# A perceiver layer on one NeuronCore: the loads' order at the start, and the experts' second products with tokens on the rows

## The chip, the core and the metric

The kernel runs on one NeuronCore of a Trainium2 chip. The core has five engines with instruction queues of their own: TensorE (PE; its weight loads are listed apart as PEld), VectorE (DVE), ScalarE (ACT), GpSimd (POOL) and SyncE (SP). They work from SBUF, 128 partitions (rows) wide; TensorE writes to PSUM, eight banks from which VectorE and ScalarE read. DMAs move data between HBM and SBUF; here SP and ACT issue them. An engine takes its instructions in the order of its queue, and a DMA-issuing instruction that has to wait holds up what is behind it in that queue.

The metric is the device time of one execution in microseconds (us).

## What is computed

32 sequences of 64 tokens and 256 features (2048 tokens) attend to a context of 1601 keys each, then to themselves with a Gaussian-like span per head, and then pass through a feed-forward part with one shared expert and eight routed ones. In the reference's words, shortened:

```python
x = x + xattn(layernorm(x), ctx, ctx, mask, ...)      # 16 heads of 16; q, k, v, o with biases
x = x + attn(layernorm(x), W_span, W_val, W_out)       # scores = -soft * (pos - mean)**2
x = x + ffn(layernorm(x), ...)

# ffn, over the tokens n = 0 .. 2047
shared = silu(xf @ sw1 + sb1) * (xf @ sw3 + sb3) @ sw2 + sb2
out = 0
for k in range(2):
    e = (n * 11 + k * 7919) % 8                        # the expert is a function of n % 8
    out += gelu(xf @ w1[e] + b1[e]) @ w2[e] + b2[e]
ffn = (shared + out / 2) / 2
```

As the expert depends on n % 8 alone, the tokens fall into eight classes r of 256 tokens each, and a class has two experts. All arithmetic is in float32.

## The kernel before, in words

**Start.** `cst` (constants: the identity matrix among them), `cols` (biases as columns) and the first tile of x are asked for on SP; `load_square` asks for the query, key and value weights and others on ACT (L122), eight loads in all with `bo_row` and `woP` (L127, L129). Then SP asks for the mask (L328) and, in `load_context(0)`, for the first sequence's context in four pieces of 496, 372, 372 and 361 keys (`GROUPS`, L404). Tiles named `ct` hold such pieces, in five buffers. At any time up to eight of the loads can be under way; a ninth waits until an earlier one has landed.

**Cross attention.** From L571 to `order.close()` (L671) the order on PE, DVE, ACT and POOL is the order of the program text (`manual_schedule`); what is traced outside of this region may be set between its instructions by the framework's scheduler, which models each engine's time and places an instruction when its inputs would be there. `query_steps` (L370) is a generator in five steps: statistics of the tile (DVE, `spread_of`), normalising (two ACT operations), transposes on PE (L170) and a copy (L377), the query products (L382) with four ACT copies into `qbd` (L390), and a bias addition (L397). The first four steps run ahead of everything (L581 to L583). `project_keys` (L413) makes a group of keys: PE products (L419) and an ACT copy with bias into `kT` (L423). `scores` (L446) makes scores (L454), DVE adds the mask to them into `prob` (L463), `maximum` keeps a running maximum (L484). Then POOL subtracts it (L515), ACT takes exponentials (L520), and `values` (L522) multiplies by the values `v` (L530), which `project_values` makes (L435, L441). A half (one sequence, eight of the heads) is worked on while the next half's scores are made. When two sequences are done, `span_steps` (L178) takes their tile through the second attention, spread over the following stretches, with operations on all four engines (L182 to L312), and writes it to `x_kept` in HBM (L306) and, normalised and transposed, to `xfT`.

**Feed-forward.** The pools of the attention are closed, and new pools `ffn`, `hid` and three PSUM pools use their memory anew; a new tile waits only for those old tiles that lie under it (`reuse_waits="tile"`). Tiles lie in a pool in the order in which the program first asks for them. SP asks for the weights (L685). The shared expert's first products run in four quarters of the tokens, interleaved with the last tile's `span_steps` (the agenda); the last quarter (L715) waits until that tile is done, as it needs the whole of `xfT`. `expert_hidden` (L741) makes a class's hidden values for its two experts (L748, L755). `expert_out` (L759) forms the second products with features on the rows: the weights are the stationary operand, 256 tokens of the class the moving one; DVE scales by 0.25 and adds the column bias `ybias` (made at L699 to L708) into `yT`, with a stride of eight tokens (L770). At the end each of the 16 token tiles is turned back by two PE transposes (L783), added to the kept x (`xe`, one load at L738) by DVE (L785) and stored (L786).

This region has no order of its own in the text: the scheduler lays it.

Of the kernel before, what the change touches and what calls it, by code (L numbers as in the profile page):

```python
# [15 lines left out]
F32 = mybir.dt.float32  # L16
U8 = mybir.dt.uint8
AF = mybir.ActivationFunctionType
ALU = mybir.AluOpType
# [3 lines left out]
P = 128  # L23
S = 64
D = 256
H = 16
# [27 lines left out]
B_2 = B_1 + 2 * E  # L54
B_S2 = B_2 + TOPK * 2 * E
B_V = B_S2 + 2
# [3 lines left out]
def expert_of(k: int, r: int) -> int:  # L60

    return (r * PRIME + k * HASH_OFF) % E
# [16 lines left out]
def perceiver_kernel(ctx: ExitStack, tc: tile.TileContext, a: dict[str, bass.AP], out: bass.AP):  # L79
# [14 lines left out]
    def mm_bank(name: str):  # L94
        return ps_mm.tile([P, 512], F32, tag="mm", name=name)
# [3 lines left out]
    nc.sync.dma_start(out=cst, in_=a["consts"])  # L99
# [6 lines left out]
    nc.sync.dma_start(out=cols, in_=a["cols"])  # L106
# [7 lines left out]
    def load_x(t: int):  # L114
        xs[t] = work.tile([P, D], F32, tag="x", bufs=4, name=f"x{t}")
        nc.sync.dma_start(out=xs[t], in_=a["x"][t * P : (t + 1) * P, :])

    load_x(0)

    def load_square(name: str, width: int = D):  # L120
        w = const.tile([P, 2, width], F32, name=f"{name}_sb")
        nc.scalar.dma_start(out=w, in_=a[name].rearrange("(c p) o -> p c o", p=P))  # L122
        return w

    wqT, wkT, wvT = (load_square(n) for n in ("wqT", "wkT", "wvT"))
    bo_row = const.tile([P, D], F32, name="bo_row")
    nc.scalar.dma_start(out=bo_row, in_=a["bo"].partition_broadcast(P))  # L127
    woP = const.tile([P, 4, D], F32, name="woP_sb")
    nc.scalar.dma_start(out=woP, in_=a["woP"])  # L129
    wspanT = load_square("wspanT", 2 * H)  # L130
    wvalT = load_square("wvalT")
    woutT = load_square("woutT")

# [183 lines left out]
    xattn = ExitStack()  # L317
    big = xattn.enter_context(tc.tile_pool(name="big", bufs=2))
# [7 lines left out]
    with tc.tile_pool(name="mask8", bufs=1) as mp:  # L326
        m8 = mp.tile([P, NKC, S], U8, name="m8")
        nc.sync.dma_start(out=m8[:CHUNK], in_=a["maskT"])  # L328
        nc.vector.tensor_scalar(madd[:CHUNK], m8[:CHUNK], -MASKED, MASKED, ALU.mult, ALU.add)
        nc.vector.tensor_scalar(  # L330
            madd[:CHUNK, NKC - 1, :], madd[:CHUNK, NKC - 1, :], cst[:CHUNK, C_PAD : C_PAD + 1],
            None, ALU.add,
        )
# [33 lines left out]
    cts: dict[int, list] = {}  # L367
# [31 lines left out]
    def load_context(b: int):  # L399
        cts[b] = []  # L400
        for g, (c0, n) in enumerate(GROUPS):
            k0, kn = c0 * CHUNK, min(n * CHUNK, KEYS - c0 * CHUNK)
            ct = big.tile([P, 2, 4 * CHUNK], F32, tag="ct", bufs=5, name=f"ct_{b}_{g}")
            nc.sync.dma_start(  # L404
                out=ct[:, :, :kn],
                in_=a["ctxT"][b].rearrange("(c p) k -> p c k", p=P)[:, :, k0 : k0 + kn],
            )
            cts[b].append(ct)
        if b % 2 == 0 and b // 2 + 1 < NTILE:
            t = b // 2 + 1  # L410
            load_x(t)

    def project_keys(b: int, c: int, g: int):  # L413

        c0, n = GROUPS[g]
        k0, kn = c0 * CHUNK, min(n * CHUNK, KEYS - c0 * CHUNK)
        ps = mm_bank(f"pk_{b}_{c}_{g}")
        for i in range(2):
            nc.tensor.matmul(  # L419
                ps[:, :kn], lhsT=wkT[:, i, c * P : (c + 1) * P], rhs=cts[b][g][:, i, :kn],  # L420
                start=(i == 0), stop=(i == 1),
            )
        nc.scalar.activation(  # L423
            kTs[c][:, k0 : k0 + kn], ps[:, :kn], AF.Identity, bias=cols[:, B_K + c : B_K + c + 1]
        )
# [154 lines left out]
    load_context(0)  # L580
    queries = query_steps(0)  # L581
    for _ in range(4):
        next(queries)  # L583
    for g in range(len(GROUPS)):
        project_keys(0, 0, g)
    for g in range(len(GROUPS)):
        scores(0, g, BETWEEN[g])
        if g == 0:
            first_maxima(0)
        project_keys(0, 1, g)  # L590
# [92 lines left out]
    def load_weights(name: str, chunks: int, width: int, src):  # L683
        w = ffn.tile([P, chunks, width], F32, name=name)
        nc.sync.dma_start(out=w, in_=src.rearrange("(c p) o -> p c o", p=P))  # L685
        return w
# [4 lines left out]
    sw2 = load_weights("sw2_sb", NHC, D, a["sw2"])  # L691
    w1, w2 = [], []
    for e in range(E):
# [4 lines left out]
    ybias = ffn.tile([P, 2 * E], F32, name="ybias")  # L698
    nc.vector.tensor_tensor(  # L699
        ybias, cols[:, B_2 : B_2 + 2 * E], cols[:, B_2 + 2 * E : B_2 + 4 * E], ALU.add  # L700
    )
    for c in range(2):
        for _ in range(2):
            nc.vector.tensor_scalar(
                ybias[:, c * E : (c + 1) * E], ybias[:, c * E : (c + 1) * E],
                cols[:, B_S2 + c : B_S2 + c + 1], None, ALU.add,
            )
    nc.vector.tensor_scalar(ybias, ybias, 0.25, None, ALU.mult)  # L708

# [26 lines left out]
    yT = ffn.tile([P, 2, NT], F32, name="yT")  # L736
    xe = ffn.tile([P, NTILE, D], F32, name="xe")
    nc.sync.dma_start(out=xe, in_=x_kept.rearrange("t p d -> p t d"))  # L738
    yTr = yT.rearrange("p c (i r) -> p c r i", r=E)
# [19 lines left out]
    def expert_out(r: int, hids):  # L759
        py = ps_y.tile([P, 2, CL], F32, tag="y", name=f"py_{r}")  # L760
        for m in range(2):
            ms = slice(m * P, (m + 1) * P)
            terms = [(sw2[:, hc, ms], gT[:, hc, r, :]) for hc in range(NHC)]
            terms += [(w2[e][:, c, ms], hT[:, c, :]) for e, hT in hids for c in range(2)]
            for n, (w, x) in enumerate(terms):
                nc.tensor.matmul(  # L766
                    py[:, m, :], lhsT=w, rhs=x, start=(n == 0), stop=(n == len(terms) - 1)
                )
            at = m * E + r
            nc.vector.tensor_scalar(  # L770
                yTr[:, m, r, :], py[:, m, :], 0.25, ybias[:, at : at + 1], ALU.mult, ALU.add
            )
# [6 lines left out]

    for t in range(NTILE):  # L780
        ps = mm_bank(f"pf_{t}")
        for c in range(2):
            nc.tensor.transpose(ps[:, c * P : (c + 1) * P], yT[:, c, t * P : (t + 1) * P], ident)  # L783
        ot = hid.tile([P, D], F32, tag="ot", bufs=4, name=f"ot_{t}")
        nc.vector.tensor_tensor(ot, xe[:, t, :], ps[:, :D], ALU.add)  # L785
        nc.sync.dma_start(out=out[t * P : (t + 1) * P, :], in_=ot)  # L786


def laid_out(
# [7 lines left out]
    def rows(v):  # L797
        return np.asarray(v).reshape(-1, P).T

    def padded(v):  # L800
# [7 lines left out]
    b2 = np.asarray(L0_ffn_b2)  # L808
    by_class = [
        rows(b2[[expert_of(k, r) for r in range(E)]]).reshape(P, E, 2).transpose(0, 2, 1).reshape(P, -1)  # L810
        for k in range(TOPK)
    ]
    cols = [
        rows(v) for v in (L0_xattn_wq_b, L0_xattn_wk_b, L0_ffn_sb1, L0_ffn_sb3, L0_ffn_b1)
    ] + by_class + [rows(L0_ffn_sb2), padded(np.asarray(L0_xattn_wv_b)[:, None])[:, :, 0].T]
# [18 lines left out]
        "w2": np.asarray(L0_ffn_w2),  # L834
    }
# [16 lines left out]
```

## Time and profile before

| | us |
|---|---|
| median of three runs (lowest, highest) | 1680.48 (1679.57, 1681.05) |
| the profiled execution | 1680.07 |
| its span, first to last recorded event | 1678.3 |
| first TensorE matmul | 11.66 |
| first scores (L454) | 20.68 |
| last read of a context piece (L435) | about 1454.5 |
| last values (L530) end | 1506.2 |
| last quarter of the shared expert's products begins | 1563.97 |
| last second product of an expert (L766) ends | 1665.5 |

The profile is one execution, recorded by the hardware. A line of the timeline gives the start and the busy time (us), the engine, the line of the program, the operation, written and read tiles, shapes and the count of merged instructions; in square brackets how long the engine had been idle before, and what ended that. "DVE prob L463" names engine, written tile and line. The chain of waits follows the work that ended last back to the beginning. DMA-issuing instructions stand on the queues SPq and ACTq; from issue to landing a load of 256 KB took 3.7 to 4.7 us at the start, where many are under way together, and a store of 128 KB at the end 1.8 us.

In the second part of the page, the span in 40 slices of 42 us, TensorE's busy share and the clock granted to it (both in tenths) fall in one slice behind the start:

| slice | 1 | 2 to 34 | 35 | 36 | 37 to 39 | 40 |
|---|---|---|---|---|---|---|
| PE | 6 | 9 | 8 | 5 | 9 | 8 |
| PEclk | 9 | 9 | 9 | 6 | 9 | 9 |

Slice 36 lies between 1468 and 1510 us.

### The profile page before, as it was taken

The page shows a single profiled execution, that of the slowest core. Times are in us where ns is not written, and L with a number is a line of the kernel's source. Part 1 is how long each engine was busy: PE and PEld are TensorE (multiplying, and loading weights), DVE is VectorE, ACT ScalarE, POOL GpSimd, SP SyncE. Part 2 cuts the span into 40 slices and gives each one's busy share as a digit, 9 for nine tenths or more (in the row PEclk, how much of TensorE's full clock was granted, in tenths as well). Part 3 has the DMA queues.
Part 4 walks back from the last instruction along what each step waited for, and adds up shares of the span by engine and source line. Part 5 has one row for each costly group of instructions (what it writes and reads, how often), then busy time and mean ns, then how long its engine had stood idle before and what let it go on. Part 6 is the DMA issues. An engine that isn't in the chain of part 4 may idle for free.

```text
span 1678.3 us, 55766 instructions
## 1 busy us (share of the span) xinstructions
PE 1585.9 (94%) x25160; PEld 1192.8 (71%) x25160; DVE 1305.6 (78%) x2637; ACT 911.3 (54%) x1271; POOL 1105.9 (66%) x395
## 2 busy tenths in 40 slices
PE   6999999999999999999999999999999999859998
PEld 4777777777777777777777777777777777644586
DVE  4788988887888889888888888897889888873112
ACT  2555656565656656565656666555656565534210
POOL 0767767787686877677877868786768777672000
PEclk9999999999999999999999999999999999969999
DMA  4211111111111111111111111111111111003101
GB/s 131 58 40 42 33 40 40 38 42 48 41 42 47 41 36 33 41 39 38 41 48 41 42 48 41 39 38 39 37 43 32 45 42 32 2 26 117 54 0 51
DMA packets 51789, 72.50 MB, mean 43 GB/s; under 512 B 3684, under 2 KB 50912, under 8 KB 51552
## 3 DMA queue, kind: packets, MB, share of 16 engines
q1 hardware_dynamic: 49632, 66.95, 13.9%
q8 instruction: 197, 3.23, 0.8%
q10 hardware_dynamic: 1920, 2.00, 0.3%
q14 instruction: 40, 0.33, 0.1%
HBM read 64.74 MB, written 4.19 MB: 41 GB/s over the span
## 4 chain that ended last, share of the span: by engine, by line
PE 55%; DVE 38%; issue 3%; POOL 1%; DMA 1%; ACT 1%; POOLq 0%; ACTq 0%; DVEq 0%
DVE prob L463 13%; DVE mrun L484 13%; PE pk L419 12%; PE pv L435 12%; PE pvs L530 9%; PE psc L454 8%; PE py L766 3%; DVE rin L557 3%; PE p L725 2%; PE pm L491 2%; PE ph L748 2%; PE pb L506 1%; DVE least L266 1%; DVE mrun L251 1%; DVE total L271 1%
## 5 line engine op out<-in xcount | busy, mean ns | idle before, releaser
L515 POOL TENSOR_TENSOR prob<-prob,mb 124x1664 f32<-124x1664 f32 x256 | 950.3, 3731 | 330.4 <-ACT mb L510 330.4
L463 DVE TENSOR_TENSOR prob<-psc,madd 124x384 f32<-124x384 f32 (+1 forms) x1024 | 584.5, 584 | 188.7 <-PE psc L454 188.7
L484 DVE TENSOR_TENSOR mrun<-prob,mrun 124x512 f32<-124x512 f32 x704 | 484.1, 688 | 7.2 <-ACT mrun L476 4.3
L419 PE MATMUL pk<-ct,wkT_sb 128*128 128x372 f32 (+2 forms) x1024 | 406.1, 520 | 8.7 <-DVE prob L463 0.2
L520 ACT ACTIVATE prob<-prob 124x1664 f32<-124x1664 f32 x256 | 400.0, 1587 | 14.7 <-POOL prob L515 14.3
L435 PE MATMUL pv<-wvT_sb,ct 128*124 128x256 f32 (+1 forms) x1664 | 384.6, 379 | 0.0
L435 PEld LDWEIGHTS pv<-wvT_sb,ct 128*124 128x124 f32 (+1 forms) x1664 | 309.9, 186 | 77.3 <-DVE prob L463 2.4
L454 PE MATMUL psc<-qbd,kT 32*124 32x128 f32 x6656 | 298.5, 287 | 33.8 <-DVE prob L463 29.0
L423 ACT ACTIVATE kT<-pk,cols 128x372 f32<-128x372 f32 (+2 forms) x256 | 152.1, 594 | 293.8 <-PE pk L419 293.4
L454 PEld LDWEIGHTS psc<-qbd,kT 32*124 32x124 f32 x6656 | 235.3, 182 | 107.1 <-DVE prob L463 55.5
L419 PEld LDWEIGHTS pk<-ct,wkT_sb 128*128 128x128 f32 x1024 | 174.3, 190 | 112.0 <-issue 29.6
L441 ACT COPY v<-pv 124x512 f32<-124x512 f32 (+1 forms) x224 | 124.7, 557 | 215.4 <-PE pv L435 214.1
L530 PE MATMUL pvs<-prob,v 124*17 124x64 f32 x13312 | 216.0, 222 | 3.7 <-ACT prob L520 3.7
L530 PEld LDWEIGHTS pvs<-prob,v 124*17 124x17 f32 x13312 | 193.2, 99 | 29.4 <-issue 24.8
L770 DVE TENSOR_SCALAR yT<-py,ybias 128x256 f32<-128x256 f32 x16 | 10.9, 679 | 74.1 <-PE py L766 74.1
L725 PE MATMUL p<-xfT,sw_sb 128*128 128x512 f32 x128 | 58.7, 616 | 2.8 <-DMA sw_sb<-in_sw 1.4
L557 DVE RECIPROCAL rin<-pr 128x256 f32<-128x256 f32 x32 | 56.0, 1750 | 5.8 <-PE pr L553 5.8
L506 PEld LDWEIGHTS pb<-cst,mc 128*124 128x124 f32 x256 | 29.8, 135 | 35.9 <-DVE mc L498 30.1
L491 PE MATMUL pm<-cst,mx 124*128 124x124 f32 x256 | 40.7, 282 | 9.8 <-DVE mx L484 8.9
L725 PEld LDWEIGHTS p<-xfT,sw_sb 128*128 128x128 f32 x128 | 24.9, 198 | 33.8 <-issue 28.4
L484 DVE TENSOR_TENSOR mx<-prob,mrun 124x512 f32<-124x512 f32 x64 | 44.0, 687 | 2.2
L156 POOL TENSOR_TENSOR rstd_f<-ve_f,neghalf 128x1 f32<-128x1 f32 x16 | 8.8, 549 | 55.4 <-DVE ve_f L154 55.4
(138 smaller groups left out, 1224.7 us busy)
## 6 DMA issues: line engine op xcount, KB each, us to landing
ct<-in_ctxT SPq DMA_DIRECT2D x64, 372.0 KB, 3.2
ct<-in_ctxT SPq DMA_DIRECT2D x32, 496.0 KB, 3.6
ct<-in_ctxT SPq DMA_DIRECT2D x32, 361.0 KB, 3.1
w<-in_w SPq DMA_DIRECT2D x16, 256.0 KB, 7.1
x<-in_x SPq DMA_DIRECT2D x16, 128.0 KB, 2.0
x_kept<-x SPq DMA_DIRECT2D x16, 128.0 KB, 1.7
xe<-x_kept SPq DMA_DIRECT2D x1, 2048.0 KB, 8.2
out<-ot SPq DMA_DIRECT2D x16, 128.0 KB, 1.8
```

What stands on the lines that cost most here:

```text
L419: nc.tensor.matmul(ps[:, :kn], lhsT=wkT[:, i, c * P : (c + 1) * P], rhs=cts[b][g][:, i, :kn], start=(i == 0), stop=(i == 1),)
L423: nc.scalar.activation(kTs[c][:, k0 : k0 + kn], ps[:, :kn], AF.Identity, bias=cols[:, B_K + c : B_K + c + 1])
L435: nc.tensor.matmul(ps[:kn, n * D : (n + 1) * D], lhsT=cts[b][g][:, i, k0 : k0 + kn], rhs=wvT[:, i, :], start=(i == 0), stop=(i == 1),)
L441: nc.scalar.copy(vs[b % 2][:kn, 2 * u : 2 * u + n, :, :DK], ps[:kn, : n * D].rearrange("p (n h d) -> p n h d", n=n, d=DK),)
L454: nc.tensor.matmul(ps[:CHUNK, k * P : (k + 1) * P], lhsT=kTs[c][32 * j : 32 * j + 32, at : at + CHUNK], rhs=qbd[b // 2][32 * j : 32 * j + ...
L463: nc.vector.tensor_tensor(pair_of(n, j)[:, c0 : c0 + nb, :].rearrange("p k (e q) -> p k e q", e=2), ps[:CHUNK, : nb * P].rearrange("p (k e ...
L484: nc.vector.tensor_tensor(dst, block_of(n, k), run, ALU.max)
L515: nc.gpsimd.tensor_tensor(sj, sj, m[:CHUNK, j, None, :].to_broadcast([CHUNK, NKC, P]), ALU.subtract)
L520: nc.scalar.activation(pair_of(n, j), pair_of(n, j), AF.Exp)
L530: nc.tensor.matmul(pvs[32 * j : 32 * j + DK + 1, c, r, :], lhsT=v[:kn, k, 8 * c + h, :], rhs=pair_of(n, h // 2)[:kn, k, (h % 2) * S : (h % ...
L557: nc.vector.reciprocal(rin, pr[:, : 4 * S])
L725: nc.tensor.matmul(ps, lhsT=w[:, c, hs], rhs=xfT[:, c, :, at], start=(c == 0), stop=(c == 1))
```

## The change

Two edits at once.

*Start.* `load_square` takes the issuing engine. The key weights are the first load on ACT, the first context piece the first on SP; x, `cst` and `cols` follow on SP; then the query weights (ACT), two more pieces (SP), the value weights (ACT), the mask, the fourth piece, and all the rest on SP. The pool `big` and the first pieces are therefore asked for at the top of the program, so `ct` is the first tile of that pool; the mask's bytes `m8` become a tile of it too. In the order of work, each of the four key groups goes ahead of one of the first four query steps.

*Experts.* `b2`, with `sb2` as a ninth row, is loaded to all partitions as rows (`b2row`), and POOL sums the biases of each class into `brow`. The kept x is loaded in eight loads, a class each, with tokens on rows, and POOL adds `brow` to it. In `expert_out` the hidden values are the stationary operand and the weights the moving one, so products come out with tokens on rows; one DVE operation scales them and adds the row of x, and SP stores 128 rows (1 KB each, 8 KB apart) right away. `ybias`, `yT` and the transposes at the end are gone.

```diff
-    load_x(0)
-    wqT, wkT, wvT = (load_square(n) for n in ("wqT", "wkT", "wvT"))
+    wkT = load_square("wkT", nc.scalar)
+    load_piece(0, 0)
     load_x(0)
+    nc.sync.dma_start(out=cst, in_=a["consts"])
+    nc.sync.dma_start(out=cols, in_=a["cols"])
+    wqT = load_square("wqT", nc.scalar)
+    load_piece(0, 1)
+    load_piece(0, 2)
+    wvT = load_square("wvT", nc.scalar)
+    m8 = big.tile([P, NKC, S], U8, name="m8", bufs=1)
+    nc.sync.dma_start(out=m8[:CHUNK], in_=a["maskT"])
+    load_piece(0, 3)
+    woP = const.tile([P, 4, D], F32, name="woP_sb")
+    nc.sync.dma_start(out=woP, in_=a["woP"])
     bo_row = const.tile([P, D], F32, name="bo_row")
-    nc.scalar.dma_start(out=bo_row, in_=a["bo"].partition_broadcast(P))
+    nc.sync.dma_start(out=bo_row, in_=a["bo"].partition_broadcast(P))
+    wspanT = load_square("wspanT", nc.sync, 2 * H)
+    wvalT = load_square("wvalT", nc.sync)
+    woutT = load_square("woutT", nc.sync)
+    load_x(1)
...
-    load_context(0)
     queries = query_steps(0)
-    for _ in range(4):
-        next(queries)
     for g in range(len(GROUPS)):
         project_keys(0, 0, g)
+        next(queries)
...
     sw2 = load_weights("sw2_sb", NHC, D, a["sw2"])
+    b2row = ffn.tile([P, E + 1, D], F32, name="b2row")
+    nc.sync.dma_start(out=b2row, in_=a["b2"].partition_broadcast(P))
...
-    yT = ffn.tile([P, 2, NT], F32, name="yT")
-    xe = ffn.tile([P, NTILE, D], F32, name="xe")
-    nc.sync.dma_start(out=xe, in_=x_kept.rearrange("t p d -> p t d"))
+    brow = ffn.tile([P, E, D], F32, name="brow")
+    for r in range(E):
+        nc.gpsimd.tensor_tensor(
+            brow[:, r, :], b2row[:, expert_of(0, r), :], b2row[:, expert_of(1, r), :], ALU.add
+        )
+    for _ in range(2):
+        nc.gpsimd.tensor_tensor(
+            brow, brow, b2row[:, None, E, :].to_broadcast([P, E, D]), ALU.add
+        )
+    nc.gpsimd.tensor_scalar(brow, brow, 0.25, None, ALU.mult)
+    xe = ffn.tile([P, E, 2, D], F32, name="xe")
+    kept_rows = x_kept.rearrange("t p d -> (t p) d").rearrange("(h p r) d -> r p h d", h=2, r=E)
+    out_rows = out.rearrange("(h p r) d -> r h p d", h=2, r=E)
+    for r in range(E):
+        nc.sync.dma_start(out=xe[:, r], in_=kept_rows[r])
+        nc.gpsimd.tensor_tensor(
+            xe[:, r], xe[:, r], brow[:, r, None, :].to_broadcast([P, 2, D]), ALU.add
+        )
...
-            terms = [(sw2[:, hc, ms], gT[:, hc, r, :]) for hc in range(NHC)]
-            terms += [(w2[e][:, c, ms], hT[:, c, :]) for e, hT in hids for c in range(2)]
+            terms = [(gT[:, hc, r, hs], sw2[:, hc, :]) for hc in range(NHC)]
+            terms += [(hT[:, c, hs], w2[e][:, c, :]) for e, hT in hids for c in range(2)]
...
-            nc.vector.tensor_scalar(
-                yTr[:, m, r, :], py[:, m, :], 0.25, ybias[:, at : at + 1], ALU.mult, ALU.add
-            )
+            ot = hid.tile([P, D], F32, tag="ot", bufs=4, name=f"ot_{r}_{h}")
+            nc.vector.scalar_tensor_tensor(ot, py[:, h, :], 0.25, xe[:, r, h, :], ALU.mult, ALU.add)
+            nc.sync.dma_start(out=out_rows[r, h], in_=ot)
...
-    for t in range(NTILE):
-        ps = mm_bank(f"pf_{t}")
-        for c in range(2):
-            nc.tensor.transpose(ps[:, c * P : (c + 1) * P], yT[:, c, t * P : (t + 1) * P], ident)
-        ot = hid.tile([P, D], F32, tag="ot", bufs=4, name=f"ot_{t}")
-        nc.vector.tensor_tensor(ot, xe[:, t, :], ps[:, :D], ALU.add)
-        nc.sync.dma_start(out=out[t * P : (t + 1) * P, :], in_=ot)
```

## The prediction

> **What bounds the kernel now.** I read the page first, then the timeline of the first 50 us, then the timeline and the chain of waits of the last 200 us, then the DMA queue's own waits. The page:
>
> ```profile
> PE 1585.9 (94%) x25160; PEld 1192.8 (71%) x25160; DVE 1305.6 (78%) x2637; ACT 911.3 (54%) x1271; POOL 1105.9 (66%) x395
> ```
>
> TensorE is busy nearly throughout, but the change touches only the two ends. Between about 45 and 1450 us a fixed order repeats, and the chain of waits passes the same piece in every second batch at an even distance (start, us, piece):
>
> ```profile
> 645.04 1.68 DVE rin L557
> 736.59 1.68 DVE rin L557
> ```
>
> 91.55 us for two batches, 16 times. None of its instructions is edited, so I carry it over unchanged and look for what each end gives.
>
> The start (timeline; start, us, engine, line, what; in brackets the idle time before and its releaser):
>
> ```profile
> 9.21 1.28 ACT L162 ACT_TABLE_LOAD   x1 [9.21 <-DMA bo_row<-in_bo]
> 11.66 0.69 PE L170 MATMUL tr_q<-cst,xn_q 128*128 128x128 f32 x2 [11.66 <-DMA woP_sb<-in_woP]
> 14.73 6.02 PE L419 MATMUL pk<-ct,wkT_sb 128*128 128x496 f32 x16
> 14.98 1.51 ACT L390 ACTIVATE qbd<-pq,bq,own 128x128 f32<-128x128 f32 x4 [3.37 <-PE pq L382]
> 20.68 1.15 PE L454 MATMUL psc<-qbd,kT 32*124 32x128 f32 x32
> ```
>
> Nothing runs on TensorE for 11.66 us: ScalarE issues eight loads and can't normalise before its last issue, at 9.1. The query's path (transposes, projections) comes first, then all four key groups, so the first scores start at 20.68.
>
> The last stage: the shared experts' weights are asked for only when the last values are done (waits of the DMA queue; total us, times, longest),
>
> ```profile
> SPq L685 <- PE pvs L530: 82.3, 1, 82.3
> ```
>
> and around that moment (timeline):
>
> ```profile
> 1489.12 12.80 DVE L704 TENSOR_SCALAR ybias<-ybias,cols 128x8 f32<-128x8 f32 x4
> 1494.53 7.37 POOL L515 TENSOR_TENSOR prob<-prob,mb 124x1664 f32<-124x1664 f32 x2
> 1494.62 1.97 PE L281 MATMUL psa<-cst,sc 128*128 128x128 f32 x8 [7.37 <-POOL sc L273]
> 1501.96 0.18 DVE L708 TENSOR_SCALAR ybias<-ybias 128x16 f32<-128x16 f32 x1
> 1510.11 3.70 PE L725 MATMUL p<-xfT,sw_sb 128*128 128x512 f32 x8 [1.38 <-DMA sw_sb<-in_sw]
> 1513.64 1.89 PE L182 MATMUL po<-woP_sb,oT 128*128 128x256 f32 x8
> ```
>
> TensorE idles 7.37 us on GpSimd, then 1.38 us for weights; from 1510 to the experts' end it is the bound except for 5 to 8 us around 1560 (the last tile's chain). The end (chain of waits):
>
> ```profile
> 1661.03 0.69 DVE yT L770
> 1661.72 0.04 issue
> 1661.76 3.73 PE py L766 x16
> ...
> 1665.52 0.69 DVE yT L770
> ...
> 1675.19 0.42 DVE ot L785
> ```
>
> After the last product (1665.49) come 12.8 us of turning, adding and storing, four stores in flight at a time.
>
> **The change, part by part.**
>
> *Keys first.* By the table of two-microsecond stretches 0.50 MB arrive between 2 and 4 us and 0.73 MB between 4 and 6 (248 and 367 GB/s). In before, the ScalarE and SP queues share this about equally: 0.99 MB had come in all when the second ScalarE load landed (1.23 + 4.1 = 5.3). So in the new order the keys' weights (0.26 MB, first on ScalarE) land at about 4.0; the first context piece (0.50 MB, first on SP, the same from the other queue beside it) at 5.3; x at 6.0, constants 6.9, columns 7.0, the second piece 8.0, the third 9.1, mask 9.4, the fourth 10.4. Then:
> - The first key group starts at 5.3. Here the skill speaks against the change: "TensorE: Matmul & The Clock Gate", Part 1, says that an idle array starts at half clock and needs about 3.4 us of activity. The page's clock row shows full speed at the start, but the rows side with the rule: the first key matmul took 1034 ns against a median of 476, the first two transposes 0.69 us against 0.38 later. At full clock the group's four passes of 496 columns take 1.65 us (0.41 each), by the rule 3.3. I take 3.3: until 8.6. As the second piece lands only at 8.0, the difference costs about 0.6 us, not 1.65.
> - Second group, half of it cold, until 10.4 (4 x 0.31 us for 372 columns when warm); its bias copy on ScalarE until 11.1, which in the new order stands ahead of the two normalising copies (0.51 each): 12.2. Statistics, 2 us from x or from the mask additions that may stand ahead of them on VectorE, are ready by then. Transposes to 12.7, copy (0.42) to 13.1; the fourth group runs meanwhile to 13.9; query products to 15.6 (8 x 0.2); two of the four qbd copies (0.38 each) to 16.4. First scores at 16.4 instead of 20.68: **4.2 us**. Ends: 2.5 if the mask holds up the statistics or all four copies are waited for, 5.5 if the cold start hides wholly.
> - Everything behind has the same order and inputs that landed before use (the values' weights by 7, the mask 7 us before the first addition, woP, asked for behind it, 15 us before its use at about 28), so the shift is carried on.
>
> *Memory order.* The context buffers are now the first tiles of the big pool, where the mask sums and the probabilities were; the two weights sw1 and sw3 then lie over context buffers (last read 1454.5) and no longer over the probabilities (1506). So SP can issue both some 50 us earlier. At least the 1.38 us wait goes. More: the first eight products of L725 (3.45 us at full clock) need only these weights, xfT of old tiles and two PSUM banks that are free by 1484; the planner already lets later work into such gaps (ybias, L699 to L704, stands ahead of L557). If it puts the eight into the 7.37 us idle time, L182 follows at 1510.2 (oT, L560) instead of 1513.64: **3.3 us** (it can't use the 1.38 twice, as L182 waits for oT). More can't move: activations write over a values tile read until 1506. Ends: 0 and 4.8. I take the upper part, because a free engine with ready work is what the planner looks for.
>
> *Biases.* The six ybias operations (14.4 us) go from VectorE while it waits for nothing but L557: worth 0. GpSimd gets, by rows: 8 additions of 256 columns (L397: 0.73) 5.8; two of 2048, between 1.86 ns a column (L258, 1024 in 1.90) and 2.24 (L515, 1664 in 3.73): 8.4 of 7.6 to 9.2; a scalar product of 2048, no row on this engine: 1.9 (half an addition) to 4.6, I take 3.8 as near L258; 8 additions of 512 (between the rows of 256 and 1024) 1.15 each, 9.2. Sum **27 us**. The skill speaks against this too: "GPSIMD Engine Reference", 1. Specifications, says that it shares its SBUF interface with VectorE, contending with two-port modes and with two SBUF inputs. The trace agrees: the four tiny L704 took 12.80 us beside L515, L708 0.18 with GpSimd idle. By the rule alone, 18 us of sums in front of the last tile's chain could hold VectorE for up to 18 us. But L237 to L253 took 0.16 to 0.27 each beside L515 at 1461 as well: they keep an operand in PSUM, as do L730 and the new addition. So by the rows 0. What remains is GpSimd's own order: the b2 rows (1.18 MB, 3.4 us at 345 GB/s) land near 1513, the 18 us run until about 1531, L258 comes at 1529.7 (1533.0 less 3.3). Allowed: 0 to 4.5 us (one operation in the way; ScalarE's order passes it on to TensorE, as the 1.04 us before the act at 1543.6 shows); I take 0, as the last key of this chain, L273, has 10 us until TensorE takes it.
>
> *Loads and stores.* The b2 rows push the experts' weights from 1524 to 1528; first use 1579.7: 0. The kept rows become eight loads of 256 KB, issued by SP at 0.37 to 0.9 each behind the last x_kept; 8.2 us to landing for 2 MB in before: by 1571, the additions behind them by about 1575, used first near 1587: 0, with 12 us of cover. Stores now go every 5.3 us, each 1.8, four buffers: no wait but the last.
>
> *Products.* Same number, weights 128x128 and 256 columns: 0. The VectorE step after each half falls from 0.68 (L770, scattered stores) to 0.45 (from L785's 0.42 and 0.48 worked from L730: 0.75 less 256 columns at 0.96 GHz, the skill's "VectorE: DVE Perf Modes", Specifications). It now waits for GpSimd's row too; behind it on VectorE stand only its likes, and TensorE's other half, which shares the bank, waits for it. In the chain the second half takes 3.63 instead of 3.45 us seven times; the last time 0.75 of pure wait. 7 x 0.18 + 0.24 = **1.5 us**.
>
> *Tail.* 32 transposes, 16 additions and waiting stores go. From the last VectorE end (1675.61) to the span's end are 2.69 us. New: 1665.52 + 0.45 + 2.69 = 1668.66 against 1678.30: **9.6 us**.
>
> Sum: 4.2 + 3.3 + 1.5 + 9.6 = 18.6 us. From the profiled execution's own 1680.07 (span 1678.3 and 1.8 around it): 1661.5; the runs' median is 0.4 above it: **1662 us**.
>
> **Rivals.**
> 1. *The eight products stay* where they are, and only the tail, the start and at most 1.4 us count: 1664 to 1665. For it: the planner's model of arrivals is not in the trace.
> 2. *GpSimd's sums in the way* of L258, L263, L267, one operation each (up to 4.5): 4 to 8 us back, 1666 to 1670. For it: 2048-column operations are the longest on that queue and the chain has no slack at L269, where ScalarE's Silu waits behind. Against: the sums are nearly done by then.
> 3. *The end's chain shortens more* (the 5 to 8 us idle near 1560 closes): 1656.
> 4. *Slower.* All big tiles move, and so does everything that reads them. If the repeated stage ran 1.4 us longer in each 91.55 (1.5%), 16 x 1.4 = 22 us would outweigh the gain: 1684. It decides from that point. Against it: five context buffers, five probability places and yet L435 took 379 ns at least, in the middle and at most, L515 3684 to 3787: the place of a tile doesn't show.
> 5. That it doesn't do what it says: transposes and yT are plainly gone, so only the start could fail, 1666.
>
> **Chances.** Forecast 0.56, rival 1 0.20, rival 2 0.12, rival 3 0.05, rival 4 0.04, rival 5 0.03. The range of the first three with the ends of the start: 1655.5 to 1669. A change within 0.2% (3.4 us) can't be told from none: faster 0.95, same 0.015, slower 0.035.
>
> **What would show it.** First matmul at 5 to 6 us, and it is L419 (in the new file its like); first scores near 16.4; sw1's issue near 1450 and not behind the last values; eight products of the shared experts before the last values; GpSimd's 19 new operations between about 1510 and 1575, small VectorE operations still at 0.2; no transposes at the end and a span end 3.2 us behind the last product. Wrong would make it: a repeated stage off 91.55, a wait for xe before the additions, or scores after 18.

## The result, and the profile after

The changed kernel took 1662.72 us (median of 4 runs, 1661.10 to 1663.97) beside 1680.03 us (4 runs, 1678.27 to 1681.05) for the kernel before: a ratio of 0.9898, 95% interval 0.9880 to 0.9915. The forecast was 1662. The profiled execution took 1663.97 with a span of 1662.2, 16.1 us shorter than the span before. The sum was met, but two of its terms were far off with opposite signs: this is what the experiments are about.

New line numbers: L427 makes key groups, L462 scores, L538 values; L721 is the shared experts' first product (L725 before), L725 its Silu, L726 the product behind it. The last tile's chain on GpSimd is L279, L284, L288, L294 (before L258, L263, L267, L273). L779 is the second product (before L766), L783 the step behind it.

The start, in the timeline of the changed kernel (start, us, engine, line, what; in brackets the idle time before and its releaser):

```profile
5.69 7.51 PE L427 MATMUL pk<-ct,wkT_sb 128*128 128x496 f32 x12 [5.69 <-DMA wkT_sb<-in_wkT]
8.20 1.28 ACT L431 ACT_TABLE_LOAD   x1 [8.20 <-DMA cols<-in_cols]
9.15 0.50 PEld L427 LDWEIGHTS pk<-ct,wkT_sb 128*128 128x128 f32 x2 [1.31 <-DMA ct<-in_ctxT]
11.98 0.57 ACT L431 ACTIVATE kT<-pk,cols 128x372 f32<-128x372 f32 x1 [1.81 <-PE pk L427]
12.45 0.50 ACT L183 ACTIVATE xn_q<-x,neg_q 128x256 f32<-128x256 f32 x1
17.04 1.15 PE L462 MATMUL psc<-qbd,kT 32*124 32x128 f32 x32 [0.90 <-ACT qbd L405]
```

TensorE begins 6 us earlier, with the keys, and the first scores come at 17.04 instead of 20.68. The 1.31 us for which the weight loads (PEld) wait for the second context piece cost TensorE next to nothing: the four passes of the first key group begin 0.83 to 0.99 us apart, against 0.42 in the next sequence (18.13), and fill the time to 9.16. The second group's begin 0.61 to 0.77 us apart, the third's 0.31. So the second group's copy comes late (11.98), and ScalarE normalises (12.45) only behind it.

Around the last stage, the waits of SP's DMA queue (us in total, times, longest):

```profile
SPq L691 <- PE pvs L538: 61.7, 1, 61.7
SPq L691 <- PE pv L443: 19.9, 1, 19.9
```

The first shared weights are now held by L443, the last reader of a context piece, and not by the last values: they are asked for at 1439.8, 63 us ahead of the end of the last values. The wait for the last values that is left (61.7 us) now holds the third ones, `sw2`, and the bias rows behind them. Then the timeline:

```profile
1504.65 3.60 PE L721 MATMUL p<-xfT,sw_sb 128*128 128x512 f32 x8
1508.08 1.89 PE L203 MATMUL po<-woP_sb,oT 128*128 128x256 f32 x8
...
1517.39 9.11 POOL L739 TENSOR_TENSOR brow<-brow,b2row 128x2048 f32<-128x2048 f32 x2
1526.59 5.37 POOL L742 TENSOR_SCALAR brow<-brow 128x2048 f32<-128x2048 f32 x1
1527.14 0.16 DVE L268 SCALAR_TENSOR_TENSOR mean<-held,rden 128x16 f32<-128x16 f32 x1
1531.94 1.90 POOL L279 TENSOR_TENSOR sc<-cst,mean 128x1024 f32<-128x1024 f32 x1
...
1535.55 1.98 PE L721 MATMUL p<-xfT,sw_sb 128*128 128x512 f32 x4 [1.24 <-ACT act L725]
1538.87 1.98 PE L721 MATMUL p<-xfT,sw_sb 128*128 128x512 f32 x4 [1.33 <-DVE gT L726]
1543.28 13.98 PE L721 MATMUL p<-xfT,sw_sb 128*128 128x512 f32 x28 [2.42 <-ACT act L725]
...
1557.97 0.60 PE L779 MATMUL py<-sw_sb,gT 128*128 128x256 f32 x2
1559.22 1.13 PE L779 MATMUL py<-sw_sb,gT 128*128 128x256 f32 x4
1561.05 2.32 PE L779 MATMUL py<-sw_sb,gT 128*128 128x256 f32 x10
1564.66 14.00 PE L721 MATMUL p<-xfT,sw_sb 128*128 128x512 f32 x32 [0.38 <-DVE xfT L333]
```

and, between L721's start and the last quarter, the chain of waits:

```profile
1502.85 8.37 DMA b2row<-in_b
1511.29 2.09 POOL brow L735 x3
...
1530.16 1.77 issue
1531.94 1.91 POOL sc L279
...
1543.28 13.98 PE p L721 x28
```

Four things are to be read here. L721 starts with no wait, 5.46 us earlier than before (1510.11), but behind the last values and ahead of L203, as before. L279 has its mean at 1527.30 and starts at 1531.94, when GpSimd has done its sums; the chain comes to it from the load of the bias rows, through all of the sums. ScalarE, whose order has L279's follower (L283) and later the exponential (L290) ahead of a Silu, and VectorE, whose order has the minimum (L287) ahead of a product (L726), pass this on to TensorE: three stalls, 4.99 us together, where before there was one of 1.04. And ahead of the last quarter 16 second products (L779) run in what was idle time.

The last quarter starts at 1564.66, 0.69 us later than before: the whole lead is gone. The end, in the chain of waits (start, us, piece) and in the timeline:

```profile
1578.67 6.91 PE ph L761 x32
...
1655.21 3.73 PE py L779 x16
```

```profile
1658.97 0.42 DVE L783 SCALAR_TENSOR_TENSOR ot<-py,xe 128x256 f32<-128x256 f32 x1 [3.81 <-PE py L779]
```

The last product ends at 1658.94 (before 1665.49), and 3.26 us follow it instead of 12.81.

The span's difference, taken apart at these points (the ledger, below):

| | predicted us | measured us |
|---|---|---|
| start (to the end of the last values, 1506.27 to 1502.36) | 4.2 | 3.9 |
| memory order (L721's start beyond that) | 3.3 | 1.55 |
| GpSimd's sums (L721's start to the last quarter's) | 0 | -6.15 |
| shared products ahead of the last quarter: 2.36 in the quarter (16.36 to 14.00), 3.45 later | not foreseen | 5.81 |
| other products (short waits of TensorE among the experts') | 1.5 | 1.44 |
| tail | 9.6 | 9.55 |
| sum | 18.6 | 16.1 |

### The profile page after: what moved, and what is told of

It is laid out like the page before. It is cut to its first block, busy times and chain, and to the rows that moved or that the text cites. A ratio compares the mean times of both kernels' runs of the same rounds, so it can differ in the third digit from the quotient of the medians.

```text
span 1662.2 us, 55706 instructions
## 1 busy us (share of the span) xinstructions
PE 1579.8 (95%) x25128; PEld 1189.2 (72%) x25128; DVE 1280.0 (77%) x2615; ACT 910.8 (55%) x1271; POOL 1137.7 (68%) x414
## 4 chain that ended last, share of the span: by engine, by line
PE 55%; DVE 38%; POOL 2%; issue 2%; ACT 1%; DMA 1%; ACTq 0%; DVEq 0%; SPq 0%
DVE prob L471 13%; DVE mrun L492 13%; PE pk L427 13%; PE pv L443 12%; PE pvs L538 9%; PE psc L462 8%; PE py L779 3%; DVE rin L565 3%; PE pm L499 2%; PE p L721 2%; PE ph L761 2%; PE pb L514 1%; DVE least L287 1%; DVE mrun L272 1%; DVE total L292 1%
## 5 line engine op out<-in xcount | busy, mean ns | idle before, releaser
L523 POOL TENSOR_TENSOR prob<-prob,mb 124x1664 f32<-124x1664 f32 x256 | 952.3, 3739 | 328.6 <-ACT mb L518 328.6
L427 PE MATMUL pk<-ct,wkT_sb 128*128 128x372 f32 (+2 forms) x1024 | 409.0, 523 | 14.3 <-DMA wkT_sb<-in_wkT 5.7
L443 PE MATMUL pv<-wvT_sb,ct 128*124 128x256 f32 (+1 forms) x1664 | 384.6, 379 | 0.0
L443 PEld LDWEIGHTS pv<-wvT_sb,ct 128*124 128x124 f32 (+1 forms) x1664 | 309.9, 186 | 77.3 <-DVE prob L471 2.4
L462 PE MATMUL psc<-qbd,kT 32*124 32x128 f32 x6656 | 298.5, 287 | 34.3 <-DVE prob L471 28.9
L462 PEld LDWEIGHTS psc<-qbd,kT 32*124 32x124 f32 x6656 | 235.3, 182 | 107.3 <-DVE prob L471 52.7
L427 PEld LDWEIGHTS pk<-ct,wkT_sb 128*128 128x128 f32 x1024 | 174.8, 190 | 119.2 <-issue 30.9
L538 PE MATMUL pvs<-prob,v 124*17 124x64 f32 x13312 | 216.6, 222 | 3.7 <-ACT prob L528 3.7
L538 PEld LDWEIGHTS pvs<-prob,v 124*17 124x17 f32 x13312 | 193.7, 99 | 29.5 <-issue 24.9
L565 DVE RECIPROCAL rin<-pr 128x256 f32<-128x256 f32 x32 | 55.9, 1746 | 20.5 <-PE pr L561 20.5
L721 PE MATMUL p<-xfT,sw_sb 128*128 128x512 f32 x128 | 58.5, 611 | 5.4 <-ACT act L725 3.7
L783 DVE SCALAR_TENSOR_TENSOR ot<-py,xe 128x256 f32<-128x256 f32 x16 | 6.8, 424 | 73.1 <-PE py L779 73.1
L721 PEld LDWEIGHTS p<-xfT,sw_sb 128*128 128x128 f32 x128 | 24.4, 194 | 36.3 <-issue 27.4
L177 POOL TENSOR_TENSOR rstd_f<-ve_f,neghalf 128x1 f32<-128x1 f32 x16 | 8.8, 550 | 56.9 <-DVE ve_f L175 56.9
```

Source lines behind the costliest of these rows:

```text
L427: nc.tensor.matmul(ps[:, :kn], lhsT=wkT[:, i, c * P : (c + 1) * P], rhs=cts[b][g][:, i, :kn], start=(i == 0), stop=(i == 1),)
L443: nc.tensor.matmul(ps[:kn, n * D : (n + 1) * D], lhsT=cts[b][g][:, i, k0 : k0 + kn], rhs=wvT[:, i, :], start=(i == 0), stop=(i == 1),)
L462: nc.tensor.matmul(ps[:CHUNK, k * P : (k + 1) * P], lhsT=kTs[c][32 * j : 32 * j + 32, at : at + CHUNK], rhs=qbd[b // 2][32 * j : 32 * j + ...
L523: nc.gpsimd.tensor_tensor(sj, sj, m[:CHUNK, j, None, :].to_broadcast([CHUNK, NKC, P]), ALU.subtract)
L538: nc.tensor.matmul(pvs[32 * j : 32 * j + DK + 1, c, r, :], lhsT=v[:kn, k, 8 * c + h, :], rhs=pair_of(n, h // 2)[:kn, k, (h % 2) * S : (h % ...
L565: nc.vector.reciprocal(rin, pr[:, : 4 * S])
```

## The experiments

Eleven kernels; each ran beside the kernel before on its chip, and ratios are to those runs (medians 1679.87 to 1680.58 us). Diffs are against the changed kernel.

### Each half of the change alone

*Start only*: the changed start, with the experts of before.

```diff
-            terms = [(gT[:, hc, r, hs], sw2[:, hc, :]) for hc in range(NHC)]
+            terms = [(sw2[:, hc, ms], gT[:, hc, r, :]) for hc in range(NHC)]
...
+        nc.tensor.transpose(ps[:, c * P : (c + 1) * P], yT[:, c, t * P : (t + 1) * P], ident)
```

> The start of the change alone, experts as before. If the two parts add up and the start is carried to the end: 3.9 us from the keys-first order (up to the last values) and 1.5 us from the shared experts' weights that are there early, so 1674.6 us, with TensorE's L725 right behind the last products of tile 14 and no wait for sw. The rival, that the last tile's chain (L258 to L273) swallows what comes before it: 1677 to 1680, with a longer wait before the last quarter.

Measured: 1673.77 us, ratio 0.9965 (0.9951 to 0.9979).

*Experts only*: the start of before, with the changed experts.

```diff
-    wkT = load_square("wkT", nc.scalar)
-    load_piece(0, 0)
     load_x(0)
...
+    wqT, wkT, wvT = (load_square(n) for n in ("wqT", "wkT", "wvT"))
...
+    for _ in range(4):
+        next(queries)
```

> The experts' part alone, start as before. If the parts add up: the whole change's 1662.7 plus the start's 5.4, so 1668 us; first scores again at 20.7, the wait for sw again 1.4, the tail 3.3 us from the last product. If the start only paid because it made room for GpSimd's sums (or the sums cost more with the later start): above 1670.

Measured: 1670.02 us, ratio 0.9942 (0.9928 to 0.9957). The two timelines, start only first, at the first and the last of the shared products:

```profile
1504.22 3.60 PE L733 MATMUL p<-xfT,sw_sb 128*128 128x512 f32 x8
...
1556.90 0.44 PE L193 MATMUL tr_f<-cst,xn_f 128*128 128x128 f32 x2 [2.60 <-ACT xn_f L186]
```

```profile
1511.12 3.70 PE L713 MATMUL p<-xfT,sw_sb 128*128 128x512 f32 x8 [1.50 <-DMA sw_sb<-in_sw]
...
1549.91 12.28 PE L713 MATMUL p<-xfT,sw_sb 128*128 128x512 f32 x28 [2.42 <-ACT act L717]
```

The wait for the weights belongs to the old start, the stall of 2.42 us to the new experts; the gap of 2.60 us in front of the last tile's transposes, filled in the changed kernel, belongs to the old experts. The parts' gains, 0.35% and 0.58%, make 0.93%, beside 1.02% for the whole: they add, within the intervals. The experts alone came 2.0 us above their forecast of 1668, to where its rival begins ("above 1670"); the 1.5 us between 0.93% and 1.02% can't be told from none here.

### What GpSimd's sums cost

The prediction counted the sums at nothing. Four ways of making them differ in how long GpSimd is busy ahead of L279. First, all three kinds on VectorE:

```diff
-        nc.gpsimd.tensor_tensor(
+        nc.vector.tensor_tensor(
             brow[:, r, :], b2row[:, expert_of(0, r), :], b2row[:, expert_of(1, r), :], ALU.add
...
-    nc.gpsimd.tensor_scalar(brow, brow, 0.25, None, ALU.mult)
+    nc.vector.tensor_scalar(brow, brow, 0.25, None, ALU.mult)
```

> The whole change, but the bias sums (L735 to L742) on VectorE instead of GpSimd. Theory: GpSimd's 20 us of sums stand before L279 of the last tile, which starts 4.6 us late, and TensorE pays for it with stalls (5.0 us against 1.0) and some 2 us of half clock: without them 1657 to 1659 us, stalls near 1 us, and no half clock at 1543. Rival: that loss comes from the chain's own operations and TensorE's order, or 9 us of sums on VectorE hold up gT just as much: 1662 to 1664.

Measured: 1657.28 us, ratio 0.9865 (0.9851 to 0.9880). Its timeline:

```profile
1519.03 1.22 DVE L742 TENSOR_SCALAR brow<-brow 128x2048 f32<-128x2048 f32 x1
...
1526.24 1.90 POOL L279 TENSOR_TENSOR sc<-cst,mean 128x1024 f32<-128x1024 f32 x1 [12.96 <-DVE mean L268]
...
1537.58 12.28 PE L721 MATMUL p<-xfT,sw_sb 128*128 128x512 f32 x28 [0.86 <-ACT act L725]
```

GpSimd idles 12.96 us and takes L279 as soon as the mean is there; one stall of 0.86 us is left. VectorE made in 1.22 us the scaling that took GpSimd 5.37.

Then, to learn whether one long operation or their total stands in the way, the same work on GpSimd in pieces of a class:

```diff
-    for _ in range(2):
-        nc.gpsimd.tensor_tensor(
-            brow, brow, b2row[:, None, E, :].to_broadcast([P, E, D]), ALU.add
-        )
-    nc.gpsimd.tensor_scalar(brow, brow, 0.25, None, ALU.mult)
+    for r in range(E):
+        for _ in range(2):
+            nc.gpsimd.tensor_tensor(brow[:, r, :], brow[:, r, :], b2row[:, E, :], ALU.add)
+        nc.gpsimd.tensor_scalar(brow[:, r, :], brow[:, r, :], 0.25, None, ALU.mult)
```

> The changed kernel, but the two additions of 2048 columns and the scalar product of 2048 columns are made class by class, 24 operations of 256 columns, still on GpSimd. Theory A: the cost of the sums is the order of GpSimd's queue, a small operation of the last tile's chain (L279) behind one 5.37 us scalar product. With pieces of about 0.7 us at most one stands in front: stalls before the last quarter back to about 1 to 2 us instead of 5.0, the shared products at full clock again, 1657.5 to 1659.5 (near the 1657.3 of the sums on VectorE). Rival B: GpSimd's sheer time, or what it takes from VectorE beside it, is the cost: as the sums' total stays some 20 to 23 us, 1662 to 1664. A third, C: the scheduler now lays many pieces ahead of L279 as it laid one long one: 1661 to 1663, with L279 as late as before.

Measured: 1664.49 us, ratio 0.9904 (0.9889 to 0.9919). Theory A of this run fell. The timeline:

```profile
1530.34 2.78 POOL L740 TENSOR_TENSOR brow<-brow,b2row 128x256 f32<-128x256 f32 x4
1533.08 1.67 POOL L741 TENSOR_SCALAR brow<-brow 128x256 f32<-128x256 f32 x2
1534.72 1.90 POOL L279 TENSOR_TENSOR sc<-cst,mean 128x1024 f32<-128x1024 f32 x1
```

Every piece stands ahead of L279, and in pieces the sums take 23.4 us instead of 20.0; L279 is 7.3 us behind its mean. So it is the total that counts. That makes a forecast for a smaller total: the shared row doubled once and added once.

```diff
-    for _ in range(2):
-        nc.gpsimd.tensor_tensor(
-            brow, brow, b2row[:, None, E, :].to_broadcast([P, E, D]), ALU.add
-        )
+    nc.gpsimd.tensor_tensor(b2row[:, E, :], b2row[:, E, :], b2row[:, E, :], ALU.add)
+    nc.gpsimd.tensor_tensor(
+        brow, brow, b2row[:, None, E, :].to_broadcast([P, E, D]), ALU.add
+    )
```

> The changed kernel, but the shared expert's bias row is doubled first (256 columns) and added once instead of twice (2048 columns each): 3.85 us less on GpSimd, the same instructions on the other engines in the same order. Theory: all of the sums stand ahead of L279 in GpSimd's queue, so what counts is how far their end lies behind the mean's 1527.3. It was 4.6 us with 20.0 us of sums (the changed kernel) and 7.4 us with 23.4 us (sums in pieces); it should now be 0.8, L279 at 1528.1, the stalls of TensorE before the last quarter 1 to 2 us instead of 5.0, the run at 1657.5 to 1659.5. Rival: VectorE beside GpSimd, or late rows of x, carry the cost: less than 1.5 us gained, 1661 or more.

Measured: 1656.60 us (1656.10 to 1657.29), ratio 0.9859 (0.9844 to 0.9874), a little better than expected. Its timeline:

```profile
1520.57 5.37 POOL L742 TENSOR_SCALAR brow<-brow 128x2048 f32<-128x2048 f32 x1
1525.73 0.16 DVE L268 SCALAR_TENSOR_TENSOR mean<-held,rden 128x16 f32<-128x16 f32 x1
1525.98 1.90 POOL L279 TENSOR_TENSOR sc<-cst,mean 128x1024 f32<-128x1024 f32 x1
...
1537.33 12.28 PE L721 MATMUL p<-xfT,sw_sb 128*128 128x512 f32 x28 [0.98 <-ACT act L725]
```

Four totals, side by side:

| | sums on GpSimd ahead of L279, us | L279 behind its mean, us | stall in front of the 28 products, us | ratio |
|---|---|---|---|---|
| on VectorE | 0 | 0.1 | 0.86, the only one | 0.9865 |
| one addition | 16.1 | 0.1 | 0.98, the only one | 0.9859 |
| the change | 20.0 | 4.6 | 2.42, the third | 0.9898 |
| in pieces | 23.4 | 7.3 | 1.22, behind one of 3.89 | 0.9904 |

Up to about 16 us the sums are free in this stage, beyond that L279 is late by about what is added. The change paid 0.33 to 0.39% for it, 5.5 to 6.6 us (0.9898 less 0.9865 and 0.9859, times 1680); of the two, only the interval of the one addition lies wholly below that of the change. The chain of waits above names another way, which wasn't tried: the sums begin when the bias rows land, 8.4 us after SP has asked for them, and SP asks for them only behind `sw2`, when the last values are done. Of all versions, with the later ones, none has a lower ratio than this one.

### The products that nobody foresaw

With tokens on rows, the first 128 tokens of a class need only the first two quarters of `gT`, so their shared products can run before the last quarter. Turning the order of the sum about takes this away and nothing else:

```diff
-            terms = [(gT[:, hc, r, hs], sw2[:, hc, :]) for hc in range(NHC)]
-            terms += [(hT[:, c, hs], w2[e][:, c, :]) for e, hT in hids for c in range(2)]
+            terms = [(hT[:, c, hs], w2[e][:, c, :]) for e, hT in hids for c in range(2)]
+            terms += [(gT[:, hc, r, hs], sw2[:, hc, :]) for hc in range(NHC)]
```

> The whole change, but each second product begins with the routed experts' terms, so that none can run before the last tile is done: same work, other order of the sum. Theory: the 16 early products of the shared expert fill TensorE's gaps near 1560 (3.5 us) and keep its clock up for the last quarter (16 x 0.43 us less than with the half clock, 2.4 us): 1667 to 1668.6 us without them. If they only filled time that something else bounds: 1662 to 1664.

Measured: 1668.46 us, ratio 0.9932 (0.9917 to 0.9946). Its timeline:

```profile
1563.12 0.44 PE L191 MATMUL tr_f<-cst,xn_f 128*128 128x128 f32 x2 [2.63 <-ACT xn_f L184]
1563.95 15.62 PE L721 MATMUL p<-xfT,sw_sb 128*128 128x512 f32 x32 [0.38 <-DVE xfT L333]
```

The gap is open again, and the last quarter takes 15.62 us instead of 14.00. TensorE's granted clock in its first 4 us is 0.59, in the change 1.00, before 0.50: the early products fill the gap and so also keep the clock up behind it. In the traces this is 1.62 us in the quarter and 3.45 behind it, 5.1 together; as the last quarter begins 0.7 us earlier here, the two spans differ by 4.3. By the ratios of all runs the loss is 0.34%, 5.7 us, beside 5.81 in the ledger, which counts from the quarter of before, 16.36.

### The memory order, and the eight products

To undo the memory order alone, the other tiles of the pool are asked for ahead of the context pieces:

```diff
+    madd = big.tile([P, NKC, S], F32, name="madd", bufs=1)
+    prob = big.tile([P, 5, 2, NKC, P], F32, name="prob", bufs=1)
+    vs = [big.tile([P, NKC, H, DK + 1], F32, name=f"v{i}", bufs=1) for i in range(2)]
+    kTs = [big.tile([P, KPAD], F32, name=f"kT{i}", bufs=1) for i in range(2)]
     cts: dict[int, list] = defaultdict(list)
...
```

> The changed kernel, but the mask sums, the probabilities, the values and the keys are asked for in the pool ahead of the context pieces, so the memory order alone goes back. Theory: sw1's and sw3's loads are issued behind the last values again (near 1502.5), the first shared products wait 1.4 to 1.5 us for them, and nothing else moves: 1.2 to 1.8 us above the changed kernel, near 1664.2. Rival, as predicted before: 3.3 us, 1666. Rival, no effect: within 0.4 us, if the later stalls swallow the wait.

Measured: 1665.92 us, ratio 0.9910 (0.9895 to 0.9925), 0.12% or 2.0 us above the change (3.2 by the medians alone, near the rival's 3.3). The intervals overlap, so that the memory order is worth more than nothing rests on the trace, where the wait is back:

```profile
1505.74 3.70 PE L721 MATMUL p<-xfT,sw_sb 128*128 128x512 f32 x8 [1.80 <-DMA sw_sb<-in_sw]
```

The other half of that step, eight products moved ahead of the last values, didn't happen. Was it the hand-written order of the attention that kept them out? Here it ends earlier:

```diff
+    order.close()
     exponentials(last, 3)
     values(last, 0)
     values(last, 1)
...
-    order.close()
```

> The changed kernel, but the hand-written order ends ahead of the last half's last exponentials and values, so the scheduler is free to set the first eight shared products between them. If the hand-written order kept them out: L721 before 1500, the run 1.5 to 3.5 us shorter, 1659 to 1661. If the scheduler itself sets them behind (its model of the weights' arrival or of the free banks): L721 at 1504 to 1506 as before, within 0.7 us of the changed kernel.

Measured: 1662.42 us, ratio 0.9889 (0.9873 to 0.9906). The timeline:

```profile
1498.52 2.96 PE L538 MATMUL pvs<-prob,v 124*17 124x64 f32 x100 [2.95 <-ACT prob L528]
1501.95 0.70 PE L561 MATMUL pr<-o,cst 128*128 128x256 f32 x2 [0.47 <-ACT o L558]
1502.49 1.03 PE L322 MATMUL po<-woutT_sb,o2T 128*128 128x256 f32 x4
1503.35 3.60 PE L721 MATMUL p<-xfT,sw_sb 128*128 128x512 f32 x8
```

The scheduler was free, TensorE idled 2.95 us with the weights long in place, and L721 still stands behind the last values. The hand-written order isn't the reason in the stretch that this frees. What in the scheduler's model it is (arrival of the weights, the banks) stays open; no order written by hand for these eight was tried.

### The start's missing 0.6 us

The query's statistics and normalising go right behind the first key group:

```diff
-    for g in range(len(GROUPS)):
-        project_keys(0, 0, g)
-        next(queries)
+    project_keys(0, 0, 0)
+    next(queries)
+    next(queries)
+    project_keys(0, 0, 1)
+    next(queries)
+    project_keys(0, 0, 2)
+    next(queries)
+    project_keys(0, 0, 3)
```

> The changed kernel, but the query's first two steps (statistics, normalising) come right behind the first key group, so ScalarE normalises before it copies the second and third groups. Theory: the start's missing 0.6 us is ScalarE's order (normalising at 12.45 behind the second group's copy at 11.98, though its inputs are there at 8.5): first scores at 15.2 to 16.2 instead of 17.04, the whole run 0.8 to 1.8 us shorter, 1661 to 1662. Rival: TensorE's own half clock and the arrival of the second piece set it: within 0.4 us of the changed kernel.

Measured: 1660.88 us, ratio 0.9885 (0.9869 to 0.9902). The timeline:

```profile
10.14 0.50 ACT L183 ACTIVATE xn_q<-x,neg_q 128x256 f32<-128x256 f32 x1
15.16 1.15 PE L462 MATMUL psc<-qbd,kT 32*124 32x128 f32 x32
```

The first scores come 1.88 us earlier, though the first two key groups are about as slow as in the change. So it is ScalarE's order that passes their lateness on to the scores. What this is worth in the end isn't shown by this run. The same edit was put on the two repaired kernels, the sums on VectorE

> The bias sums on VectorE and the query's first two steps right behind the first key group together. If both gains are at different places and add up: the 1657.3 of the first less the second's 0.8 to 1.8, so 1655.5 to 1656.5. If the start's gain is swallowed later: 1657.3.

(measured 1657.06 us, ratio 0.9860, 0.9845 to 0.9874) and the one addition

> The query's first two steps right behind the first key group, and the shared expert's bias row added once in its doubled form, both on the changed kernel. If the two gains add up: 1656.6 less the 1.9 us by which the first scores came earlier, so 1654.5 to 1655.5. If the start's gain is swallowed later, as the 0.8 us between the runs with the sums on VectorE without and with it let one fear: 1656 to 1657.

(measured 1656.65 us, ratio 0.9862, 0.9845 to 0.9878). The gain is 2.2, 0.8 and -0.5 us by the three pairs of ratios, and in each pair the intervals overlap. In the traces the lead can be followed at L565, which begins once in each sequence. At its first time, near 91 us, the eight profiles with the changed start gave 91.34 to 92.45, the three with the earlier query 90.58 to 90.61: 1.2 us of lead in the mean, and a spread of 1.1 us among the eight, though up to there they have the same order. The spread arises in the first 12 us: the third key group begins at 10.61 to 11.78 in the eight, as the first group starts at 5.34 to 5.94 and the passes of the second take 1.35 to 2.62 us; from there to L565 seven of them need 80.67 to 80.69 us, start only 80.84. At the last values the lead of the last pair is 0.45 us, at the first shared product 0.09. So the path of the miss is shown, and the edit's gain is too small beside the spread to be told.

## Why the prediction was right in the sum, and where it was not

**Start, 4.2 us forecast, 3.9 by the end of the last values.** The mechanism holds. The first scores came at 17.04, not 16.4. The slow first group was rightly counted: 3.47 us (forecast 3.3), from 5.69 instead of 5.3. The second, forecast as half slow at 1.8 us, took 2.62 from its first pass to the third group's, so its copy ended at 12.55 instead of 11.1 and the normalising behind it at 13.55 instead of 12.2. What of this was left at the scores is 0.6 us. In the other profiles with this start the second group took 1.35 to 2.56 us, so the forecast lies within what happens.

**Memory order, 3.3 forecast, 1.55 measured: a mis-sized term.** The wait for the weights went, as forecast. That the planner "puts the eight into the 7.37 us idle time" was an assumption about the scheduler with no row behind it, and it failed: rival 1's order is what happened. That "a free engine with ready work is what the planner looks for" was no ground; ending the hand-written order didn't change it either.

**Biases at 0: the step that failed.** The price of the operations was fair: 20.0 us of sums up to L742 against 18.0 forecast. VectorE's small operations stayed at 0.16 to 0.27 us beside them, as the rows had said. The failure is in the last clause, "I take 0, as the last key of this chain, L273, has 10 us until TensorE takes it". The slack of the chain's end says nothing of what hangs on its middle: ScalarE holds the Silu of TensorE's next products behind its operations on what L279 and L288 make, and VectorE a product behind the minimum. The prediction knew that path, from the 1.04 us of before, and put the price of it, 4 to 8 us, into rival 2 with a chance of 0.12. Besides, the sums were 4.6 us in the way and not one or two. The forecast's "until about 1531" and 1529.7 leave out the lead of the start; less its 3.9 us they are 1527.1 and 1525.8. The mean came at 1527.3, 1.5 us behind that, the sums' end at 1531.96, 4.9 behind it: the bias rows landed at 1511.29, 2.2 us later than "near 1513" less 3.9, the sums took 2.0 us more, and a step of the last tile stood among them (L177, 0.55). The 6.15 us are three parts. The stalls rose by 3.95 us. The 28 products behind them took 13.98 us instead of 12.28, at a granted clock of 0.63 in their first 4 us instead of 1.00. And 36 products that ran in one piece before, in 15.72 us, are broken up into 28, 4 and 4, of 12.28, 1.98 and 1.98: 0.52 us more.

**Not foreseen: 5.8 us from products that became ready earlier.** "Products. Same number, weights 128x128 and 256 columns: 0" looked at durations and not at what each product waits for. With features on rows, a product took all 256 tokens of a class, from all four quarters; with tokens on rows its first half waits for two of them. The edit was named, its effect on readiness wasn't. Of the 5.8 us, 3.45 are the products themselves and 2.36 the faster last quarter behind them. Rival 3, the gap near 1560 closing, was this, without the mechanism.

**Products 1.5 and tail 9.6: 1.44 and 9.55.** Both steps are right in their parts: the seven passages of 3.63 us are 3.45 now, VectorE's last step took 0.42 us (forecast 0.45), loads of x and their additions ended at 1577, 10 us ahead of their use.

**Rival 4 fell:** two batches still take 91.56 us (the changed kernel's L565 at 271.44 and 363.00), and GpSimd's long operation 3739 ns in the mean against 3731.

The forecast stands at 0.7 us from the median because -6.15 and +5.81 cancelled: that is luck. In the profiled executions the sum was 16.1 us and not 18.6. The rivals 1, 2 and 3, each given less than the forecast, all took place together.

## What to carry to other kernels

When work moves to an engine that is half idle, don't ask whether its last instruction is in time: list what is queued behind the moved work on that engine, and for each of these what waits on every other engine's queue. When the operands of a product change roles, work out anew which inputs each product needs and when they are there; this can be worth more than what the change was counted for. A sum that comes out right confirms no term of it: compare the two traces at fixed points, a term at a time.

## What was not expected of the hardware

- GpSimd's scaling of 128x2048 by a constant took 5.37 us, longer than its addition of two operands of that size, 4.52; VectorE took 1.22 and 2.29 (two in 4.61). In pieces of 256 columns it is 0.85 each, eight for 6.7 us; the forecast, from two-operand rows, was 3.8. Groups of the changed kernel, 1500 to 1580 us (times and mean ns of one):

```profile
L739 POOL TENSOR_TENSOR brow<-brow,b2row 128x2048 f32<-128x2048 f32 x2 | 9.0, 4516 | 0.2
L742 POOL TENSOR_SCALAR brow<-brow 128x2048 f32<-128x2048 f32 x1 | 5.4, 5372 | 0.1
```

- The price of a stall differs between executions. Behind nearly the same three stalls (0.59 to 1.29, then 1.33 and 2.42 or 2.43 us) the 28 products took 13.98 us in the change, with the sum turned about and with the order ended earlier, at a granted clock of 0.57 to 0.63 in their first 4 us; in the experts alone and with the earlier query they took 12.28, at 1.00. So 1.7 us of the change's 6.15 may not be there in each execution. The Trainium skill, "TensorE: Matmul & The Clock Gate", Part 1, has a free-running activity window and calls the number of slow products run-variable, which fits; the page's advice to avoid gaps of more than some 3 us ("Why this matters for your kernels") doesn't suffice here, as none of these stalls is that long.
